# The bias of v folded into its weights, and the turn of x of batch 1 issued at other places: a linear-attention block with a feed-forward layer

## The chip, the cores and the metric

The kernel runs on one core of a Trainium2 chip. The metric is the device time of one execution in microseconds. A time is the median of several executions; the profile comes from one further execution, which has its own time and, inside it, its span from the first to the last instruction.

## The reference

All arithmetic is in float32. There are 8 batches of 1024 tokens with 256 channels; attention has 16 heads of 16 channels, and the hidden layer has 1024 channels.

```
xn  = (x - mean(x)) / sqrt(var(x) + 1e-5)              # over the 256 channels
q, k, v = split(xn @ qkv_w + qkv_b)                    # heads of 16
q, k = q / max(|q|, 1e-12), k / max(|k|, 1e-12)        # per token and head
kv  = sum over tokens of k[d] * v[e]                   # 16 x 16 per head
att = (q @ kv, heads joined) @ proj_w + proj_b
ffn = relu(xn @ W1 + b1) @ W2 + b2
out = x + att + ffn
```

There is no softmax. So the attention of a batch is `q` times one 256x256 matrix M = blockdiag(kv) @ proj_w, and the sum over tokens can be taken before the weights of v are applied.

## The kernel before, in words

Tokens lie on the 128 partitions in 8 tiles of 128 rows (`NT`); the 256 channels are two chunks of 128 (`KC`). The normalised x (`xn`, tokens on partitions, one buffer) is turned into `xnT` (channels on partitions, two buffers), which feeds the matmuls of the projections and of the hidden layer. The large products are split in 2x2 blocks and use seven block products in place of eight; the sums of blocks that this takes (`sums_of_a`, `sums_of_b`) are done by GpSimdE.

The program is written under a manual schedule: each engine gets its instructions in the order of the program text, and semaphores are set where data or buffers require them. The loop over batches `b` does, in this order: `hidden(b)` (first layer with relu, in 12 steps), `project(b + 1)` or `project_by_sums(b + 1)` (q and k of the next batch), and `second(b)` (second layer and `q @ M` in one accumulation), which is a generator in two parts, so that statistics, normalisation and turn of batch b + 2 and `mix_g(b + 1)` are issued between these parts.

The 12 steps of `hidden` (numbered from 0) are `first(0)`, `fifth(0)`, `first(1)`, `last(0)`, `fifth(1)`, `first(2)`, `last(1)`, `fifth(2)`, `first(3)`, `last(2)`, `fifth(3)`, `last(3)`. `first(i)` issues three block products into banks a, c, d, with a ScalarE copy `u1` and two VectorE adds; `fifth(i)` issues one into bank e with a VectorE add and a relu on ScalarE; `last(i)` completes a, d, e, with two VectorE adds and three relus. Behind each step the small work that a table names for it is issued: `first_steps` for batch 0 and `later_steps` for the others. In batch 0 this small work holds the whole normalisation of batch 1 (`norm_stats`, `norm_scale`, `norm_apply`), its turn (`turn_x`) and the mixing of batch 0.

The mixing of a batch has these parts. `sum_of_k` adds the normalised k over the tiles on GpSimdE, into `ksum` (128 x 256). `mix_g` forms G = xn^T k on TensorE (L492, `gp`) and copies it to `gT` on ScalarE. `mix_kv` forms v's side: for each of the two chunks a matmul of the bias of v with `ksum` (L505), and two of v's weights with `gT` (L509), all into `kvp`; VectorE then keeps the blocks of the heads. `mix_m` multiplies by proj_w.

`turn(dst, src, name, queues)` turns a 128 x 1024 pair of chunks in four parts: for each j a VectorE transpose of 32 x 32 blocks into a buffer (L291), and four transfers that move its row groups r to their places (L293). It is a generator, and `turn_x` issues one j for each call. A transfer is issued by an engine's queue, which stands still for that time. In the kernel before, the transfers of r = 1 and 3 are issued by ScalarE's queue for batch 1, and all others by SP:

```
turns["x", b] = turn(xnTs[b], xns[b], f"x_{b}", (nc.sync, nc.scalar if b == 1 else nc.sync))
```

The banks of PSUM are one pool of seven and one of one (for `gp`, `kvp`, `mp`).

Of the kernel before, what the change touches and what calls it, by code (L numbers as in the profile page):

```python
# [9 lines left out]
F32 = mybir.dt.float32  # L10
AF = mybir.ActivationFunctionType
ALU = mybir.AluOpType
# [4 lines left out]
def kernel(  # L17
# [10 lines left out]
    b2: bass.AP,  # L28
    out: bass.AP,
):  # L30

# [16 lines left out]
    nc = tc.nc  # L50
    P = 128
    B, N, C = x.shape
# [6 lines left out]
    KC = C // P  # L59
# [3 lines left out]
    R = P // S  # L63
# [5 lines left out]
    const = ctx.enter_context(tc.tile_pool(name="const", bufs=1))  # L69
    big = ctx.enter_context(tc.tile_pool(name="big", bufs=2))  # L70
    one = ctx.enter_context(tc.tile_pool(name="one", bufs=1))
# [20 lines left out]
    xs, xqs, xns, xnTs, xSs, hTs, qks, qTs, mixes, Ms, hSs = ({} for _ in range(11))  # L92
# [67 lines left out]
    make_identity(nc, ident)  # L160
    eps_sb = const.tile([P, 1], F32, tag="eps", name="eps_sb")
    nc.vector.memset(eps_sb, LN_EPS)

    blk = const.tile([P, G], F32, tag="blk", name="blk")
    nc.vector.tensor_reduce(blk, ident.rearrange("p (g d) -> p g d", d=D), AX.X, ALU.add)
# [69 lines left out]
    def norm_stats(b, tiles):  # L235

        xt, n = xs[b], len(tiles)
        st = work.tile([P, NT, 6], F32, tag="st", name=f"st_{b}_{tiles[0]}")[:, :n, :]
        mv = small.tile([P, NT, 2], F32, tag="mv", name=f"mv_{b}_{tiles[0]}")[:, :n, :]
        for i, t in enumerate(tiles):  # L240
            nc.vector.bn_stats(st[:, i, :], xt[:, t, :])
        for i in range(n):
            nc.vector.bn_aggr(mv[:, i, :], st[:, i, :])
        rstd = small.tile([P, NT], F32, tag="rstd", name=f"rstd_{b}_{tiles[0]}")[:, :n]
        nc.scalar.activation(rstd, mv[:, :, 1], AF.Sqrt, bias=eps_sb)
        for i, t in enumerate(tiles):
            stats[b, t] = i, mv, rstd

    def norm_scale(b, tiles, on_act):
        i, mv, rstd = stats[b, tiles[0]]  # L250
        nc.vector.reciprocal(rstd, rstd)
        if on_act:
            nmr = small.tile([P, NT], F32, tag="nmr", name=f"nmr_{b}_{i}")[:, : len(tiles)]
            nc.vector.scalar_tensor_tensor(nmr, mv[:, :, 0], -1.0, rstd, ALU.mult, ALU.mult)
            for t in tiles:
                stats[b, t] += (nmr,)
# [25 lines left out]
                    tp.rearrange("p (u w) m -> p u w m", w=2),  # L282
                )

    def turn(dst, src, name, queues=(nc.sync, nc.sync)):


        sq = one.tile([P, R, KC, NP, S, 2], F32, tag="turn", name=f"turn_{name}")
        src = src[:, :, 0:C].rearrange("p (u w) (k j s) -> p j k u w s", w=2, k=KC, s=S)
        for j in range(R):  # L290
            nc.vector.transpose(sq[:, j, :, :, :, :].rearrange("p k u s w -> p k u w s"), src[:, j])  # L291
            for r in range(R):
                queues[r % 2].dma_start(  # L293
                    out=dst[ts(j, S), :, :, ts(r, S), :], in_=sq[ts(r, S), j, :, :, :, :]
                )
            yield
# [3 lines left out]
    def turn_x(b):  # L300

        if b not in xnTs:
            xnTs[b] = big.tile([P, KC, NP, P, 2], F32, tag="xnT", name=f"xnT_{b}")
            turns["x", b] = turn(
                xnTs[b], xns[b], f"x_{b}", (nc.sync, nc.scalar if b == 1 else nc.sync)
            )
        next(turns["x", b])

    def project(b, between={}, with_norms=True):
# [164 lines left out]
            turns["q", b] = turn(qTs[b], qks[b], f"q_{b}")  # L474
        next(turns["q", b])

    def sum_of_k(b):
        qk = qks[b]

        ksum = one.tile([P, 2, C], F32, tag="ksum", name=f"ksum_{b}")  # L480
        nc.gpsimd.tensor_tensor(ksum, qk[:, 0:2, C : 2 * C], qk[:, 2:4, C : 2 * C], ALU.add)
        nc.gpsimd.tensor_tensor(ksum, ksum, qk[:, 4:6, C : 2 * C], ALU.add)
        nc.gpsimd.tensor_tensor(ksum, ksum, qk[:, 6:8, C : 2 * C], ALU.add)
        nc.gpsimd.tensor_tensor(ksum[:, 0], ksum[:, 0], ksum[:, 1], ALU.add)
        mixes[b] = [ksum]

    def mix_g(b):
        qk, xn = qks[b], xns[b]
        gp = ps_mix.tile([P, KC, C], F32, tag="mix", name=f"gp_{b}")
        for f in range(KC):  # L490
            for t in range(NT):
                nc.tensor.matmul(  # L492
                    gp[:, f, :], xn[:, t, ts(f, P)], qk[:, t, C : 2 * C],
                    start=(t == 0), stop=(t == NT - 1),
                )
        gT = one.tile([P, KC, C], F32, tag="gT", name=f"gT_{b}")
        nc.scalar.copy(gT, gp)
        mixes[b].append(gT)

    def mix_kv(b):  # L500
        ksum, gT = mixes.pop(b)
        kvp = ps_mix.tile([P, KC, P], F32, tag="mix", name=f"kvp_{b}")
        for c in range(KC):
            cols = slice(2 * C + c * P, 2 * C + (c + 1) * P)
            nc.tensor.matmul(  # L505
                kvp[:, c, :], qkvb_sb[:, cols], ksum[:, 0, ts(c, P)], start=True, stop=False
            )
            for f in range(KC):
                nc.tensor.matmul(  # L509
                    kvp[:, c, :], wqkv_sb[:, f, cols], gT[:, f, ts(c, P)],  # L510
                    start=False, stop=(f == KC - 1),
                )
        kvm = one.tile([P, KC, P], F32, tag="Mt", name=f"kvm_{b}")
        for c in range(KC):
            nc.vector.tensor_tensor(
                kvm[:, c, :].rearrange("p (g d) -> p g d", d=D),
                kvp[:, c, :].rearrange("p (g d) -> p g d", d=D),
                blk.unsqueeze(2).to_broadcast([P, G, D]), ALU.mult,
            )
        mixes[b] = kvm  # L520

    def mix_m(b):
        kvm = mixes.pop(b)
        mp = ps_mix.tile([P, KC, C], F32, tag="mix", name=f"mp_{b}")
        for c in range(KC):
            nc.tensor.matmul(mp[:, c, :], kvm[:, c, :], projw_sb[:, c, :], start=True, stop=True)  # L526
        M = one.tile([P, KC, C], F32, tag="M", name=f"M_{b}")
        Mt = one.tile([P, 3, HC], F32, tag="Mt", name=f"Mt_{b}")
        Ms[b] = M, Mt
        nc.vector.tensor_copy(M, mp)  # L530
        sums_of_b(
            nc.gpsimd, [M[:, k, ts(m, HC)] for k in range(2) for m in range(2)],
            [Mt[:, i, :] for i in range(3)],
        )
# [93 lines left out]
    def first_steps(b):  # L628

        lo, hi = range(HT), range(HT, NT)  # L630
        return {
            0: [lambda: load_squares(b)] + [lambda h=h: norms(b, h, all_ss[b, h]) for h in range(2)],
            1: [lambda: sum_of_k(b), lambda: norm_stats(b + 1, lo)],
            2: [lambda: norm_stats(b + 1, hi), lambda: norm_scale(b + 1, lo, True)],
            4: [
                lambda: mix_g(b), lambda: norm_scale(b + 1, hi, False),
                lambda: norm_apply(b + 1, lo), lambda: scale_q(b, 0), lambda: scale_q(b, 1),
            ],
            5: [lambda: norm_apply(b + 1, hi)],
            6: [lambda: mix_kv(b)],  # L640
            7: [lambda: turn_x(b + 1), lambda: turn_x(b + 1)],
            8: [lambda: turn_x(b + 1), lambda: turn_x(b + 1)],
            9: [lambda: mix_m(b)],
            11: [lambda: load(b + 2)],
        }

# [14 lines left out]
    def sums_of_q(b):  # L661
        sums_of_a(
            nc.vector if b == B - 1 else nc.gpsimd,
            halves(qTs[b]), *(hSs[b][:, s, FH] for s in range(3)),
        )
# [148 lines left out]
    for b in range(B):  # L814
        if b > 0:
            load_squares(b, (0,) if b == B - 1 else (0, 1))
            if b + 2 < B:
                load(b + 2)
        hidden(b)
        if b == 0:  # L820
            qTs[0] = one.tile([P, KC, NP, P, 2], F32, tag="qT", name="qT_0")
            turn_on_pe(qTs[0], qks[0], "q_0")
            sums_of_w2()
            sums_of_q(0)
        if b + 1 == 1:
            project(1)
            out_parts = second(b)
        elif b + 1 < B:
            project_by_sums(b + 1)
            out_parts = second(b, lambda: norms_of_q(b + 1))  # L830
        else:
            out_parts = second(b)
        next(out_parts)
        if b + 1 == 1:
            sums_of_x(1, 0)
            sums_of_x(1, 1)
            sums_of_wqk()
        if b + 1 < B:
            sum_of_k(b + 1)
        if b + 2 < B:  # L840
            norm_stats(b + 2, range(NT))
            norm_scale(b + 2, range(NT), True)
        if b + 1 < B:
            mix_g(b + 1)
        if b + 2 < B:
            norm_apply(b + 2, range(NT))
            for _ in range(R):
                turn_x(b + 2)
        next(out_parts)


# [29 lines left out]
```

## Time and profile before

| what | value |
|---|---|
| times of three executions, us | 627.03, 628.73, 628.95 (median 628.73) |
| the profiled execution: time, span, us | 626.93, 624.8 |
| TensorE matmul busy in the span | 616.5 us, 99% |
| VectorE busy | 399.7 us, 64% |
| GpSimdE busy | 385.4 us, 62% |
| ScalarE busy | 199.7 us, 32% |
| mean busy share of the 16 DMA engines on SP's and ScalarE's queue | 26.4% and 0.3% |
| granted TensorE clock | 0.999 |

PE is TensorE's matmul side, PEld its weight load, DVE VectorE, ACT ScalarE, POOL GpSimdE and SP the engine whose queue issues transfers. In a row, the arrow points from what is read to what is written, in the program's names; a count follows an x; in a timeline, the bracket tells how long the engine was idle before and what released it. In the chain of work that ended last, each row is a stretch of one engine that the end of the run depended on, with its start and length. Rows with "q" behind an engine are its queue, where transfers are issued. An f32 matmul of the program appears as two matmul records.

### The profile page before, as it was taken

Reading aid. Unit: us, or ns where it says so; the run is one execution under the profiler, and the core shown is the slowest. Engines: PE = TensorE matmul, PEld = TensorE weight load, DVE = VectorE, ACT = ScalarE, POOL = GpSimd, SP = SyncE. Lnnn points to the kernel's source line nnn. Section 1 sums busy time; section 2 is a strip of 40 time slices with the busy share of each in tenths; the row PEclk is TensorE's granted clock in tenths of the full one; section 3 lists DMA queues with packets and bytes.
Section 4 is the critical chain, followed back from the end, with each engine's and each line's share of the span. In section 5 each row is a group of like instructions: output and inputs, shape, how many; then the busy total and the mean of one; then the engine's idle time right before and its main releaser. Section 6 shows DMA issues by size and latency. Waiting matters only on the chain.

```text
span 624.8 us, 6180 instructions
## 1 busy us (share of the span) xinstructions
PE 616.5 (99%) x1873; PEld 348.0 (56%) x1873; DVE 399.7 (64%) x696; ACT 199.7 (32%) x340; POOL 385.4 (62%) x320
## 2 busy tenths in 40 slices
PE   8998999999999999999999999999999999999996
PEld 5464455556545666447564484644846557555454
DVE  6785725677647766577566874667845678417833
ACT  4354403352033521244231432315223252103500
POOL 3575949399534994259932797329954299543801
PEclk9999999999999999999999999999999999999999
DMA  7624001460015500264003710046100450004202
GB/s 254 118 58 134 3 0 29 124 175 11 0 50 134 154 2 0 65 156 117 0 1 100 190 47 0 5 123 175 36 0 22 122 125 2 0 1 101 67 1 67
DMA packets 139504, 43.28 MB, mean 69 GB/s; under 512 B 135880, under 2 KB 136272, under 8 KB 139472
## 3 DMA queue, kind: packets, MB, share of 16 engines
q1 hardware_dynamic: 137296, 42.37, 26.4%
q10 hardware_dynamic: 2176, 0.52, 0.3%
q8 instruction: 15, 0.25, 0.2%
q14 instruction: 17, 0.14, 0.1%
HBM read 19.80 MB, written 8.39 MB: 45 GB/s over the span
## 4 chain that ended last, share of the span: by engine, by line
PE 97%; DVE 1%; DMA 1%; ACT 0%; issue 0%; SPq 0%; ACTq 0%; DVEq 0%
PE poe L670 11%; PE poa L670 11%; PE pod L670 10%; PE gp L492 9%; PE phe L548 9%; PE pha L548 9%; PE phd L548 8%; PE poc L670 5%; PE pq L326 4%; PE phc L548 4%; PE pqa L394 3%; PE pqd L394 3%; PE pqe L394 3%; PE pqc L394 2%; PE kvp L509 1%; PE mp L526 1%
## 5 line engine op out<-in xcount | busy, mean ns | idle before, releaser
L707 POOL TENSOR_TENSOR xq<-xq,yt_o 128x512 f32<-128x512 f32 x30 | 37.9, 1264 | 145.0 <-DVE yt_o L702 145.0
L555 ACT ACTIVATE hT<-hT,b_sb 128x512 f32<-128x512 f32 x96 | 68.6, 721 | 60.3 <-DVE hT L560 55.7
L184 POOL TENSOR_TENSOR hS<-hT 128x512 f32<-128x512 f32 x31 | 46.5, 1499 | 60.7 <-ACT hT L555 60.7
L548 PE MATMUL pha<-xnT,w_sb 128*128 128x512 f32 x128 | 65.4, 592 | 0.0
L372 ACT ACTIVATE sq<-qk 128x512 f32<-128x512 f32 x48 | 29.0, 629 | 109.1 <-DVE qk L400 59.1
L670 PE MATMUL poa<-hT,w_sb 128*128 128x512 f32 x128 | 57.5, 592 | 0.0
L492 PE MATMUL gp<-qk,xn 128*128 128x256 f32 x256 | 56.6, 379 | 0.0
L492 PEld LDWEIGHTS gp<-qk,xn 128*128 128x128 f32 x256 | 48.6, 190 | 10.0 <-issue 3.8
L560 DVE TENSOR_TENSOR hT<-phe,u 128x512 f32<-128x512 f32 x64 | 43.7, 684 | 7.0 <-PE phe L548 5.3
L702 DVE STREAM_TRANSPOSE yt_o<-y_o 128x512 f32<-128x512 f32 x30 | 33.0, 1099 | 16.2 <-ACT y_o L757 13.9
L186 POOL TENSOR_TENSOR hS<-hT,hS 128x512 f32<-128x512 f32 x31 | 40.4, 1303 | 2.4
L185 POOL TENSOR_TENSOR hS<-hS,hT 128x512 f32<-128x512 f32 x31 | 40.3, 1299 | 2.4
L574 ACT COPY u<-pha 128x512 f32<-128x512 f32 x32 | 18.4, 575 | 69.5 <-PE pha L548 66.5
L188 POOL TENSOR_TENSOR hT<-hT 128x512 f32<-128x512 f32 x31 | 39.9, 1288 | 0.0
L670 PEld LDWEIGHTS poa<-hT,w_sb 128*128 128x128 f32 x128 | 24.3, 190 | 25.0 <-issue 24.4
L291 DVE STREAM_TRANSPOSE turn_x<-xn 128x512 f32<-128x512 f32 x28 | 17.6, 687 | 31.1 <-ACT xn L265 31.1
L548 PEld LDWEIGHTS pha<-xnT,w_sb 128*128 128x128 f32 x128 | 23.8, 190 | 23.8 <-issue 21.0
L560 DVE TENSOR_TENSOR u<-phc,u 128x512 f32<-128x512 f32 x32 | 21.8, 682 | 22.8 <-ACT u L574 15.0
L548 PE MATMUL phe<-xS,w_sb 128*128 128x512 f32 x64 | 32.8, 594 | 1.7 <-DVE hT L560 1.7
L555 ACT ACTIVATE hT<-pha,b_sb 128x512 f32<-128x512 f32 x32 | 21.8, 682 | 37.5 <-PE pha L548 32.4
L548 PE MATMUL phd<-xnT,w_sb 128*128 128x512 f32 x64 | 32.7, 592 | 0.0
L548 PE MATMUL phe<-xS,w1t 128*128 128x512 f32 x64 | 32.7, 592 | 0.0
(164 smaller groups left out, 1227.0 us busy)
## 6 DMA issues: line engine op xcount, KB each, us to landing
xq<-in_L_attn_x_dram SPq DMA_DIRECT2D x60, 128.0 KB, 3.0
out_dram<-xq SPq DMA_DIRECT2D x60, 128.0 KB, 2.4
x<-in_L_attn_x_dram SPq DMA_DIRECT2D x14, 512.0 KB, 6.6
qT<-turn_q SPq DMA_DIRECT2D x112, 64.0 KB, 2.1
xnT<-turn_x SPq DMA_DIRECT2D x104, 64.0 KB, 2.1
x<-in_L_attn_x_dram SPq DMA_DIRECT2D x4, 256.0 KB, 3.9
w_sb<-in_L_ffn_W_dram SPq DMA_DIRECT2D x2, 512.0 KB, 7.2
w_sb<-in_L_ffn_W_dram SPq DMA_DIRECT2D x8, 128.0 KB, 3.1
```

The lines of the kernel that those rows point to most:

```text
L184: eng.tensor_tensor(s1, a21, a22, ALU.add)
L185: eng.tensor_tensor(s2, s1, a11, ALU.subtract)
L186: eng.tensor_tensor(s4, a12, s2, ALU.subtract)
L188: eng.tensor_tensor(a21, a11, a21, ALU.subtract)
L394: nc.tensor.matmul(dst[:, w, :], a[:, g, :, w], rhs, start=start and w == 0, stop=stop, skip_group_check=True,)
L492: nc.tensor.matmul(gp[:, f, :], xn[:, t, ts(f, P)], qk[:, t, C : 2 * C], start=(t == 0), stop=(t == NT - 1),)
L548: nc.tensor.matmul(dst, lhsT, rhs, start=start, stop=stop, skip_group_check=True)
L555: nc.scalar.activation(block(i, n, m), src, AF.Relu, bias=b1_sb[:, fc : fc + 1])
L560: nc.vector.tensor_tensor(dst, p, q, ALU.add)
L670: nc.tensor.matmul(dst, l, r, start=start and n == 0, stop=stop and n == len(lhs) - 1, skip_group_check=True,)
L702: nc.vector.transpose(yt.rearrange("p u w r c -> p u r w c"), y.rearrange("p u (s r) w -> p u r w s", r=R),)
L707: nc.gpsimd.tensor_tensor(xh, xh, yt.rearrange("p u w r c -> p (u w) r c"), ALU.add)
```

## The change

The output is unchanged in meaning. A layer-normalised row sums to zero over its 256 channels. Let u be the vector with ones in the first 128 channels and zeros in the others. If 1 is added to the first 128 channels of `xn` (`shift`), `mix_g` forms G + u s^T, where s is the sum of k over the tokens. If a row `a` is added to every row of v's weights W (`fold_bias_of_v`), the product W'^T (G + u s^T) is W^T G + (W^T u + 128 a) s^T, because each column of G sums to zero over channels. With a = bias / 128 - (mean of the first 128 rows of W) this is W^T G + bias s^T, which is what the bias matmuls gave.

- `sum_of_k` and the two bias matmuls of each `mix_kv` are gone.
- `fold_bias_of_v` is issued once, behind step 3 of batch 0: a memset, one matmul and two VectorE instructions.
- `shift(b)` is one ScalarE activation over the first 128 channels of `xn`, issued once per batch: for batch 0 behind step 2, for batch 1 behind the turn of q on TensorE, for the later ones at the end of the loop's body, two batches ahead.
- The turn of x of batch 1 is issued one part behind step 7, two behind step 8 and one behind step 9 (two and two before), and only the transfer r = 3 of each part goes to ScalarE's queue.
- `mix_m` of batch 0 moves from behind step 9 to behind step 10.

```diff
+    ones = const.tile([P, 1], F32, tag="ones", name="ones")
+    nc.vector.memset(ones, 1.0)
...
-    def turn(dst, src, name, queues=(nc.sync, nc.sync)):
+    def turn(dst, src, name, last=nc.sync):
...
-                queues[r % 2].dma_start(
+                (last if r == R - 1 else nc.sync).dma_start(
...
-    def sum_of_k(b):
-        qk = qks[b]
-
-        ksum = one.tile([P, 2, C], F32, tag="ksum", name=f"ksum_{b}")
-        nc.gpsimd.tensor_tensor(ksum, qk[:, 0:2, C : 2 * C], qk[:, 2:4, C : 2 * C], ALU.add)
-        nc.gpsimd.tensor_tensor(ksum, ksum, qk[:, 4:6, C : 2 * C], ALU.add)
-        nc.gpsimd.tensor_tensor(ksum, ksum, qk[:, 6:8, C : 2 * C], ALU.add)
-        nc.gpsimd.tensor_tensor(ksum[:, 0], ksum[:, 0], ksum[:, 1], ALU.add)
-        mixes[b] = [ksum]
+    def fold_bias_of_v():
+
+        wv = wqkv_sb[:, :, of_v]
+        mean = one.tile([P, P], F32, tag="Mt", name="mean")
+        nc.vector.memset(mean, 1.0 / P)
+        of_rows = bank([P, C], "of_rows")
+        nc.tensor.matmul(of_rows, mean, wv[:, 0, :], start=True, stop=True)
+        a = one.tile([P, C], F32, tag="ksum", name="a")
+        nc.vector.scalar_tensor_tensor(
+            a, qkvb_sb[:, of_v], 1.0 / P, of_rows, ALU.mult, ALU.subtract
+        )
+        nc.vector.tensor_tensor(wv, wv, a.unsqueeze(1).to_broadcast([P, KC, C]), ALU.add)
+
+    def shift(b):
+
+        part = xns[b][:, :, 0:P]
+        nc.scalar.activation(part, part, AF.Identity, bias=ones)
...
     def mix_kv(b):
-        ksum, gT = mixes.pop(b)
+        gT = mixes.pop(b)
...
-            nc.tensor.matmul(
-                kvp[:, c, :], qkvb_sb[:, cols], ksum[:, 0, ts(c, P)], start=True, stop=False
-            )
...
-                    start=False, stop=(f == KC - 1),
+                    start=(f == 0), stop=(f == KC - 1),
...
-            1: [lambda: sum_of_k(b), lambda: norm_stats(b + 1, lo)],
-            2: [lambda: norm_stats(b + 1, hi), lambda: norm_scale(b + 1, lo, True)],
+            1: [lambda: norm_stats(b + 1, lo)],
+            2: [lambda: shift(b), lambda: norm_stats(b + 1, hi), lambda: norm_scale(b + 1, lo, True)],
+            3: [lambda: fold_bias_of_v()],
...
-            7: [lambda: turn_x(b + 1), lambda: turn_x(b + 1)],
+            7: [lambda: turn_x(b + 1)],
             8: [lambda: turn_x(b + 1), lambda: turn_x(b + 1)],
-            9: [lambda: mix_m(b)],
+            9: [lambda: turn_x(b + 1)],
+            10: [lambda: mix_m(b)],
...
             sums_of_q(0)
+            shift(1)
...
-        if b + 1 < B:
-            sum_of_k(b + 1)
...
         next(out_parts)
+        if b + 2 < B:
+            shift(b + 2)
```

More of the change, by code (lines that the diff above doesn't have):

```diff
@@ L303, in turn_x @@
             xnTs[b] = big.tile([P, KC, NP, P, 2], F32, tag="xnT", name=f"xnT_{b}")
-            turns["x", b] = turn(
-                xnTs[b], xns[b], f"x_{b}", (nc.sync, nc.scalar if b == 1 else nc.sync)
-            )
+            turns["x", b] = turn(xnTs[b], xns[b], f"x_{b}", nc.scalar if b == 1 else nc.sync)
         next(turns["x", b])
@@ L497, in mix_g @@
         nc.scalar.copy(gT, gp)
-        mixes[b].append(gT)
+        mixes[b] = gT
     def mix_kv(b):
-        ksum, gT = mixes.pop(b)
+        gT = mixes.pop(b)
         kvp = ps_mix.tile([P, KC, P], F32, tag="mix", name=f"kvp_{b}")
@@ L504, in mix_kv @@
             cols = slice(2 * C + c * P, 2 * C + (c + 1) * P)
-            nc.tensor.matmul(
-                kvp[:, c, :], qkvb_sb[:, cols], ksum[:, 0, ts(c, P)], start=True, stop=False
-            )
             for f in range(KC):
```

## The prediction

> **What bounds the kernel now.** I read the busy times first, then the chain of work that ended last, then TensorE's own waits.
>
> ```profile
> PE 616.5 (99%) x1873; PEld 348.0 (56%) x1873; DVE 399.7 (64%) x696; ACT 199.7 (32%) x340; POOL 385.4 (62%) x320
> PE 97%; DVE 1%; DMA 1%; ACT 0%; issue 0%; SPq 0%; ACTq 0%; DVEq 0%
> PE phe L548 <- DVE hT L560: 1.7, 1, 1.7
> ```
>
> TensorE is the bound: the chain is 97% PE, and after the start-up its only wait of size is one of 1.7 us. So a matmul taken out saves its time, and a matmul that waits costs its wait. The chain in order of time shows both places that the change touches:
>
> ```profile
> 44.83 0.22 PE kvp L505 x2
> 45.05 0.45 PE kvp L509 x4
> 45.50 0.22 PE kvp L505 x2
> 45.72 0.45 PE kvp L509 x4
> ...
> 47.89 1.22 DVE turn_x L291 x2
> ...
> 51.60 0.58 ACT u L574
> ...
> 57.33 1.12 PE phe L548 x2
> 58.45 1.75 PE tpq L279 x16
> 60.20 13.74 PE pq L326 x32
> ```
>
> First, the bias matmuls of `kvp` (L505) lie on the chain, 0.22 us each (an f32 matmul leaves two records). Secondly, batch 0's hidden stage leaves PE: a DVE turn, DMA issues on ScalarE, its copy `u` (L574), and DVE, until `phe` resumes at 57.33.
>
> The timeline of 24 to 75 us shows how far VectorE is behind TensorE where the new matmul is put:
>
> ```profile
> 31.75 1.02 PE L548 MATMUL phe<-xS,w1t 128*128 128x512 f32 x2
> 32.61 7.07 PE L492 MATMUL gp<-qk,xn 128*128 128x256 f32 x32
> 32.74 0.69 DVE L560 TENSOR_TENSOR u<-phc,u 128x512 f32<-128x512 f32 x1 [0.84 <-ACT u L574]
> 34.14 1.40 DVE L241 BATCH_NORM_STATS2 st<-x 128x6 f32<-128x256 f32 x4
> 36.73 1.27 DVE L560 TENSOR_TENSOR hT<-phe,u 128x512 f32<-128x512 f32 x2
> 38.01 4.20 DVE L462 TENSOR_TENSOR qk<-qk,ss 128x1024 f32<-128x1024 f32 x2
> ```
>
> TensorE ends `last(0)` at 31.91 (32.77 less the 0.86 us of `fifth(1)`); VectorE adds that step's `phe` only at 36.73 (the first of the two; the second is `fifth(1)`'s). The norm statistics of batch 1, put into steps 1 and 2, hold it up. Today nobody minds: `gp` needs nothing of it.
>
> **What the skill says.** "PSUM — Partial Sum Buffer", Engine vs sequencer instructions: the queues of ScalarE, VectorE and GpSimdE are strictly first in, first out, and matmuls keep program order. The trace agrees: every DVE row above stands in the order of the steps. "DMA: Bandwidth & Descriptors", Issuing engines are not separate DMA queues: a second issuing engine saves only issue time. Here that time is real, 0.68 us per turn transfer on SP:
>
> ```profile
> 103.49 10.93 SPq L293 DMA_DIRECT2D xnT<-turn_x  x16
> ```
>
> "TensorE: Matmul & The Clock Gate", What's actually happening: after an idle window of about 3.4 us the array runs at half speed until it has been busy for such a window. The start agrees, although the clock column says 1.00: 20 cold transposes take 226 ns apiece, 16 warm ones 109 ns by the chain (1.75/16). After the 1.7 us idle at 55.6, `tpq` was at full speed.
>
> ```profile
> 1.36 4.53 PE L786 MATMUL warm<-ident 128*128 128x128 f32 x20 [1.36 <-POOL ident masks.py:199]
> ```
>
> **The change part by part.**
>
> *Bias matmuls out.* Two per batch at 0.22 us: 0.44 x 8 = 3.5 us off PE. For batches 1 to 7 (3.1 us) PE shows no wait, so all of it counts.
>
> *Sum of kn out.* GpSimdE loses 1.27 x 3 + 0.73 = 4.5 us per batch. PE never waited on `ksum`, so this is worth nothing; the residual adds (L707) and stores come earlier, which the chain doesn't contain.
>
> *The fold, once, behind step 3 of batch 0.* It adds a memset of `mean` (DVE), a matmul `of_rows` of 256 columns (PE), then `a` and the add into `wv` (DVE). `of_rows` needs `mean`, and the memset stands in DVE's queue behind `last(0)`'s adds. These end 36.73 + 0.68 = 37.4, with the next issue about 0.6 us after the first, at 37.33. The memset of 128x128 isn't in the trace on DVE: between 0.15 us (reciprocal of 128x4) and 0.22 us (128x128 scalar op); I take 0.2. So PE, ready at 31.91, starts near 37.55 and sits idle 5.6 us with `fifth(1)` and `mix_g` behind it. `of_rows` takes 2 x 0.216 us (from 32 records of 256 columns in 6.91 us) and a restart of 0.26 (the `phe` after the wait took 1.12 instead of 0.86): it ends at 38.24. `fifth(1)` ends at 39.10, where it was 32.77: **+6.3 us**. The DVE part, 0.5 + 0.69 us (L772's and L560's rows), then runs beside `fifth(1)` and `gp`; VectorE has caught up, and its 4.2 us of `scale_q` fit under `gp`'s 6.9.
>
> Does the lateness of VectorE get paid back later by this pause? Only the wait at 55.6 could repay it, and that hangs on work behind `gp`: batch 1's normalised x reuses the single `xn` buffer, so ScalarE's copies of it (40.20 to 42.27) and its copy `u` at 42.18 follow `gp` as before. The delay carries through whole.
>
> *The array's clock.* An idle time of 5.6 us holds a whole free-running 3.4 us window with a chance of (5.6-3.4)/3.4 = 0.65. Half speed for one window costs 1.7 us. Bounds: 0, and half of the at most 5.7 us that the start was cold (1.36 to 7.05), 2.9. I take **+1.7**.
>
> *Shift.* Eight activations over 128x1024. By the trace an activation with a bias tile is 0.72 us at 512 elements; "ScalarE: Activation LUTs", What ACT_TABLE_LOAD costs, gives 280 ns + 0.833 ns per element, an estimate of 1.13 us; twice 0.72 is the upper bound. Batch 0's runs behind `u` (32.71) and ends near 33.9, under the wait for `mean`; without that wait `gp` would start 0.6 us late. Batch 1's stands behind the copies of `qT`, ahead of `project(1)`'s squares: these come 1.1 us later, with 1.1 us of ScalarE idle per tile (L332) to recover and seven banks released by DVE before them. Batches 2 to 7's wait for the last turn (105.1 in the first such stage) and end near 106.3; the next ScalarE work is at 111.84 after 8.7 us of idle. Zero.
>
> *Turn of x of batch 1.* Before: two turns behind step 7, two behind step 8, 8 transfers on SP, 8 on ScalarE. After: one, two, one, and only the fourth of each four on ScalarE, so SP issues 12. ScalarE's block ahead of `u` falls from 2.94 us to about 0.7. In the clock of before: turn 0 at 47.81, `u` at 49.3, DVE's two adds to 51.2, turns 1 and 2 to 52.5, `last(2)`'s adds to 53.7, turn 3 to 54.3, `fifth(3)`'s add to 54.9. TensorE, 0.44 us earlier by `kvp`, needs that add at 55.17: the 1.71 us wait goes. But then `tpq` ends at 57.8, and `project(1)` needs all 16 transfers. SP: three at 48.5 to 50.6, then nine from 51.9 at 0.68 us, the last issued at 57.3, landing 2.1 us later (their median): 59.4, perhaps 59.7. Before, `project(1)` began at 60.04. So 1.7 us are won and about 1.7 paid again for SP's queue; beyond the 0.44 of `kvp`, **0** (bounds -1.7 and +1). The move of `mix_m` behind step 10 is free: nothing needs M before the output stage.
>
> Sum: 6.3 + 1.7 - 3.5 + 0 = **+4.5 us**. Against the profiled execution (span 624.8, time 626.93) this is 631.4; that execution lies 1.8 under the median of the three runs, so against the median it is 633.2. With the clock spared it is 631.5.
>
> **Rivals.**
> *No wait for `mean`.* VectorE reaches the memset before PE needs it. Then `of_rows` costs 0.43, `gp` waits 0.6 for the shift, and the sum is 1.05 - 3.5 = -2.5 us: **626.2**. It decides as soon as VectorE is less than some 2 us behind at the end of `last(0)`. Against it: the 36.73 of the trace, and no earlier place in a first-in-first-out queue. For it: only that the issue order need not be that of the text.
>
> *The wait, but all else goes well.* The clock stays up and the transfers land before `tpq` ends: 6.3 - 3.5 - 1.7 = +1.1 us, **629.8**. For it: landing times as short as 2.0 us; against it: 12 issues at 0.68 are 8.2 us from 48.5.
>
> *SP worse than reckoned.* Transfers of two queues held each other up before (SP's fourth was issued 1.8 us late, put down to a transfer). Were that so with one ScalarE issue per turn, `project(1)` starts 1 to 2 us later still: **635**.
>
> **How the numbers follow.** Forecast 0.66 (with or without the clock penalty 631.5 to 634.5), worse SP 0.12, all going well 0.09, no wait 0.13. A difference of 0.3% (1.9 us) is about what can be told from none. Faster 0.13, same 0.09, slower 0.78. The range 629.7 to 635.6 leaves out the no-wait rival and the tails.
>
> **What would show it.** In the profile after: a PE wait of about 5.6 us at `of_rows`, released by the memset; `gp` of batch 0 starting near 39.1, or its first records at half speed; no L505 rows; the PE wait on L560 gone and a wait of `pq` on the turn's transfers in its place; stages of batches 1 to 7 of 74.8 us, where they were 75.3. I am wrong if `of_rows` runs straight behind `last(0)` at about 32 us.

## The result, and the profile after

| | before | after |
|---|---|---|
| median of six executions each, us | 627.06 (626.96 to 628.95) | 633.82 (633.43 to 635.73) |
| profiled execution: time, span, us | 626.93, 624.8 | 633.63, 631.8 |
| granted TensorE clock, mean over the span | 0.999 | 0.994 |

The kernel after is slower: the ratio of the times is 1.0105, with a 95% interval of 1.0086 to 1.0124, and the medians differ by 6.8 us. GpSimdE is busy for 349.0 us where it had 385.4 us, and 32 instructions fewer; TensorE's busy time is the same, although 16 bias matmuls are gone. The page, busy times of after:

```profile
PE 616.4 (98%) x1843; PEld 346.4 (55%) x1843; DVE 400.4 (63%) x700; ACT 208.8 (33%) x348; POOL 349.0 (55%) x288
```

A bound engine with less work and the same busy time has worked more slowly somewhere, and its span says that it has waited too. TensorE's waits in after (what waited, for what; us in total, times, the longest):

```profile
PE of_rows L485 <- DVE mean L483: 5.5, 1, 5.5
PE pq L328 <- DMA xnT<-turn_x: 1.9, 1, 1.9
```

The wait on VectorE's add (L560 before) is gone from this list. In its place stand one for the turn's transfers of about the same length, and a new one of 5.5 us. The chain of work that ended last, in order of time (start, length, engine, line), where the new wait lies:

```profile
36.41 1.28 DVE hT L567 x2
37.69 0.15 DVE mean L483
37.84 0.04 issue
37.88 1.22 PE of_rows L485 x2
39.10 1.71 PE phe L555 x2
40.81 8.29 PE gp L502 x32
```

The chain goes through VectorE's two late adds, then the memset, and only then to TensorE. And the matmuls behind it are slow: `phe` takes 1.71 us where it takes 0.86 elsewhere, `gp` 8.29 where it took 6.91. The table by stretches of time (stretch; its length; the busy time of PE, PEld, DVE, ACT and POOL, each with its instructions; then the granted clock, the DMA share and the rate) says why:

```profile
32.00:38.00 6.00, 0.45 (x2) 0.12 (x1) 4.85 (x20) 3.55 (x7) 0.76 (x2) 0.89 0.48 93
38.00:40.00 2.00, 2.00 (x4) 1.30 (x5) 0.83 (x2) 0.45 (x1) 1.92 (x2) 0.50 0.03 8
40.00:42.00 2.00, 2.00 (x5) 1.21 (x5) 2.00 (x4) 0.29 (x1) 1.92 (x2) 0.50 0.00 0
42.00:44.00 2.00, 2.00 (x8) 1.64 (x7) 2.00 (x2) 0.43 (x1) 2.00 (x2) 0.63 0.00 0
44.00:46.00 2.00, 2.00 (x11) 1.77 (x10) 1.49 (x1) 0.00 (x0) 0.41 (x1) 1.00 0.00 0
```

TensorE was busy for 0.45 of the 6 us from 32 on. Its clock fell to half before that wait was over, and came back between 42 and 44 (the trace's own record: half speed from 36.66, for 6.83 us). From 37.88 to 43.49 that is 5.6 us of matmuls at half speed, so about 2.8 us lost, an estimate from these two figures. The chain has 2.76 (the table below).

Later in the chain of after:

```profile
54.25 0.89 PE kvp L516 x8
...
66.74 2.14 DMA xnT<-turn_x
68.88 0.24 issue
69.12 13.98 PE pq L328 x32
```

`kvp` is 0.89 us for a batch where it was 1.34 (two rows of 0.22 fewer). `project(1)` starts at 69.12, released by the last transfer that SP issued. From the end of `gp` to the end of `project(1)` before took 34.26 us and after 34.00.

One more difference is in no wait of TensorE's: from the last VectorE add into x (L729 before, L738 after) to the end of the span it is 4.0 us before and 4.9 after. There the last stores land (the last row of each view below). The DMA view of before (a queue's packets, MB and share of 16 engines; then issues, KB each, median us to landing):

```profile
q1 hardware_dynamic: 137296, 42.37, 26.4%
...
xq<-in_L_attn_x_dram SPq DMA_DIRECT2D x60, 128.0 KB, 3.0
out_dram<-xq SPq DMA_DIRECT2D x60, 128.0 KB, 2.4
...
out_dram<-x SPq DMA_DIRECT2D x2, 256.0 KB, 2.5
```

The same view of after:

```profile
q1 hardware_dynamic: 138384, 42.63, 30.5%
...
xq<-in_L_attn_x_dram SPq DMA_DIRECT2D x60, 128.0 KB, 3.7
out_dram<-xq SPq DMA_DIRECT2D x60, 128.0 KB, 2.8
...
out_dram<-x SPq DMA_DIRECT2D x2, 256.0 KB, 3.5
```

Transfers of the same bytes took longer: the loads of `xq`, the stores of `xq`, and the two stores at the end. What the change did to them: the new constant `ones` (128 x 1) takes 32 bytes in each partition, and the buffers placed behind it move up by 32 bytes (`x` from 77568 to 77600, `xq` from 186112 to 186144, `xnT` from 61184 to 61216). Before, these addresses were multiples of 256.

The difference of the two spans, 7.0 us, in terms that the chains show one by one:

| term | us | from |
|---|---|---|
| first transfer of x lands later (3.58 us, not 3.16) | +0.4 | start of the chain; 2.7 to 3.8 in the runs below, with no order to it |
| TensorE idle for `mean` | +5.55 | idle time at `of_rows` |
| `of_rows` itself, with restart | +0.69 | taken as forecast, since here it ran at half speed (1.22 in all); 0.70 in the filler run below |
| `of_rows`, `phe` and `gp` at half speed | +2.76 | 1.22 + 1.71 + 8.29, less 0.69 + 0.86 + 6.91 |
| end of `gp` to end of `project(1)` | -0.26 | of it -0.44 `kvp`, so +0.18 for the turn; `project(1)` itself took 13.98 in place of 13.74 after its wait |
| end of `project(1)` to the last add | -3.12 | 546.92 before, 543.80 after: 7 x 0.446 |
| last add to the end | +0.95 | 4.9 less 4.0 |

### The profile page after: what moved, and what is told of

It reads as the page before. It is cut to its first block, busy times and chain, and to the rows that moved or that the text cites. A ratio compares the mean times of both kernels' runs of the same rounds, so it can differ in the third digit from the quotient of the medians.

```text
span 631.8 us, 6102 instructions
## 1 busy us (share of the span) xinstructions
PE 616.4 (98%) x1843; PEld 346.4 (55%) x1843; DVE 400.4 (63%) x700; ACT 208.8 (33%) x348; POOL 349.0 (55%) x288
## 4 chain that ended last, share of the span: by engine, by line
PE 94%; DVE 3%; DMA 1%; ACT 0%; issue 0%; SPq 0%; DVEq 0%; ACTq 0%
PE poe L679 11%; PE poa L679 11%; PE pod L679 10%; PE gp L502 9%; PE phe L555 8%; PE phd L555 8%; PE pha L555 8%; PE poc L679 5%; PE pq L328 4%; PE phc L555 4%; PE pqd L396 3%; PE pqe L396 3%; PE pqa L396 3%; PE pqc L396 2%; PE kvp L516 1%; PE mp L533 1%
## 5 line engine op out<-in xcount | busy, mean ns | idle before, releaser
L502 PE MATMUL gp<-qk,xn 128*128 128x256 f32 x256 | 58.0, 386 | 0.0
L190 POOL TENSOR_TENSOR hS<-hT,hS 128x512 f32<-128x512 f32 x31 | 39.9, 1286 | 2.4
L189 POOL TENSOR_TENSOR hS<-hS,hT 128x512 f32<-128x512 f32 x31 | 39.5, 1274 | 2.4
```

Source lines behind the costliest of these rows:

```text
L189: eng.tensor_tensor(s2, s1, a11, ALU.subtract)
L190: eng.tensor_tensor(s4, a12, s2, ALU.subtract)
L502: nc.tensor.matmul(gp[:, f, :], xn[:, t, ts(f, P)], qk[:, t, C : 2 * C], start=(t == 0), stop=(t == NT - 1),)
```

## The experiments

All were timed beside runs of the kernel before on the same chip. Before was 627.0 us in the first group (filler, memset early, turn alone, fold in `project(0)`), 626.98 in the second (ones beside eps, fold with the old turn, filler ahead of `project(1)`, two and two) and 626.99 in the third. A figure that compares one experiment with another, or with after, can go across these groups, whose before agrees to 0.02 us. The recorded mean clock of an execution, where it is given, also holds the half speed at the end of a program, when TensorE has no more work; that alone takes up to 0.003, as in the memset moved to the start (from 623.63 to its end at 627.14).

**Theory:** VectorE's lateness at `mean` and the clock lost to that wait make the kernel slow; the saving in `kvp` is real; the turn is about neutral; the stores at the end pay for the place of `ones`. **Rivals:** the stall would have come anyway a little later (a bank, or an add at 55 us), so that the wait is repaid; the slow matmuls are not the clock; the transfers are slow for another reason than their addresses.

### The wait alone, put into the kernel before

```diff
+    def wait_for_memset():
+        mean = one.tile([P, P], F32, tag="Mt", name="mean")
+        nc.vector.memset(mean, 1.0 / P)
+        of_rows = bank([P, C], "of_rows")
+        nc.tensor.matmul(of_rows, mean, wqkv_sb[:, 0, of_v], start=True, stop=True)
+        a = one.tile([P, C], F32, tag="gT", name="a")
+        nc.vector.tensor_copy(a, of_rows)
...
+            3: [wait_for_memset],
```

> The kernel before with only the memset of mean, the matmul of_rows and a copy of its result (not used) behind step 3; the bias matmuls, ksum and the turn stay. Theory (wait and clock are the whole loss): 5.5 us idle, 0.7 for the matmul and its restart, 2.8 for the clock, together 9 us over before. Rival (the later lateness of VectorE is paid back by the pause): 7 us or less, with the wait of phe on VectorE's add gone.

Measured: 636.12 us, ratio 1.0136 (1.0118 to 1.0153), so 9.1 us. Its chain, and then TensorE's waits:

```profile
37.38 0.15 DVE mean L489
...
37.57 1.22 PE of_rows L491 x2
38.79 1.71 PE phe L556 x2
40.50 7.76 PE gp L500 x32
```

```profile
PE of_rows L491 <- DVE mean L489: 5.7, 1, 5.7
PE phe L556 <- DVE hT L568: 1.6, 1, 1.6
```

The same `of_rows` and `phe` as in after, to 0.01 us. And the wait on VectorE's add of before is still there with 1.6 us: nothing of the pause is paid back. The rival, 7 us or less without that wait, is out.

The size needs care. The table's terms give 5.55 + 0.69 + 2.76 = 9.0 us, and the median of these four executions agrees with it. The profiled one is the fastest of the four (635.21, its span 8.4 us over that of before), and its own terms are 5.65 us idle, 0.69 for `of_rows`, and 2.23 for the clock, 8.6 together: `gp` took 7.76 here and 8.29 in after. The half speed lasted 6.83 us in both, but here it began earlier, at 35.28, so that 2.3 us of it fell into the wait where after had 1.2. So the price of the clock depends on when the half speed starts.

### TensorE kept busy through the wait

```diff
         of_rows = bank([P, C], "of_rows")
+        for i in range(48):
+            nc.tensor.transpose(of_rows[:, 0:P], ident, ident)
         nc.tensor.matmul(of_rows, mean, wv[:, 0, :], start=True, stop=True)
```

> As after, but TensorE runs 48 transposes of the identity into the bank of of_rows while it would wait for the memset (48 x 0.109 = 5.2 us); they compute nothing. Theory (the idle time also costs clock): of_rows still starts at about 37.9 us, but gp takes 6.9 us in place of 8.3 and the stretch from of_rows to the end of gp is 2.8 us shorter; 2.8 us under after. Rival (the slow stretch is due to VectorE, GpSimdE and TensorE reading SBUF together): no change against after.

Measured: 630.69 us, ratio to before 1.006 (1.0044 to 1.0076), 3.1 us under after. Its chain:

```profile
37.39 0.15 DVE mean L483
...
37.58 0.70 PE of_rows L487 x2
38.28 0.86 PE phe L557 x2
39.14 6.91 PE gp L504 x32
```

`mean` is as late as in after, but TensorE is busy until 0.3 us before it, and everything behind runs at full speed. So `gp` was slow because of the clock, not because VectorE and GpSimdE read the memory beside it: during `gp` they are busy for 4.75 and 5.80 us here, and for 4.68 and 3.60 in after. From `of_rows` to the end of `gp` it is 8.47 us in place of 11.22, so the clock was worth 2.75 us; 0.3 of the 3.1 is an earlier start of `of_rows`.

### The memset at the start of the program

```diff
     nc.vector.memset(ones, 1.0)
+    mean = one.tile([P, P], F32, tag="Mt", name="mean")
+    nc.vector.memset(mean, 1.0 / P)
...
-        mean = one.tile([P, P], F32, tag="Mt", name="mean")
-        nc.vector.memset(mean, 1.0 / P)
         of_rows = bank([P, C], "of_rows")
```

> The memset of mean is issued at the start of the program, the rest is as in the kernel after. Theory (the position in VectorE's queue is the cost): the 5.5 us wait of of_rows goes, and with it the 2.8 us at half clock. Left of it: fifth(1) may wait until about 33.9 us for a PSUM bank, since of_rows now holds one that a VectorE instruction frees late (1 to 2 us). Forecast 1 to 2.5 us under before, 8 us under after. Rival (of_rows waits for a PSUM bank that ScalarE's relu or VectorE frees near 37 us, and the memset only happened to come at that time): of_rows still waits about 5 us and the time stays within 1 us of after.

Measured: 628.98 us, ratio 1.0027 (1.002 to 1.0035): 4.8 us under after, but not under before, which was expected. Its waits on TensorE:

```profile
PE pq L330 <- DMA xnT<-turn_x: 3.2, 1, 3.2
...
PE phe L555 <- DVE u L567: 1.1, 1, 1.1
```

The wait at `of_rows` is gone. `fifth(1)` then waits 1.1 us for a bank that VectorE frees, and `gp` runs from 34.69 at full speed. What was missed lies at `project(1)`: it waits 3.2 us for the turn's transfers and its 32 matmuls take 15.68 us where before needed 13.74. That is the clock again: half speed from 63.84, for 3.41 us, which is 1.7 of the 1.94 us (the rest also shows in after, where `pq` takes 13.98 after a wait at full clock). The turn is not neutral once the pause ahead of it is gone.

### The turn alone

```diff
-                queues[r % 2].dma_start(
+                (last if r == R - 1 else nc.sync).dma_start(
...
-            7: [lambda: turn_x(b + 1), lambda: turn_x(b + 1)],
+            7: [lambda: turn_x(b + 1)],
             8: [lambda: turn_x(b + 1), lambda: turn_x(b + 1)],
-            9: [lambda: mix_m(b)],
+            9: [lambda: turn_x(b + 1)],
+            10: [lambda: mix_m(b)],
```

> The kernel before with only the turn's part of the change (one, two, one; one ScalarE transfer in four; mix_m behind step 10). Theory of the prediction (the wait moves from VectorE's add to SP's queue): within 0.5 us of before; the 1.7 us wait on VectorE's add is gone and project(1) waits 1.2 to 2 us for the transfers. Rival (the turn's part is worth its 1.7 us, and the fold alone spoils the change): 1.7 us under before, with no wait of project(1).

Measured: 629.32 us, ratio 1.003 (1.0016 to 1.0043), so 2.3 us, where at most 0.5 was expected. Its chain, and then the waits of SP's queue:

```profile
58.41 2.05 DMA xnT<-turn_x
60.45 0.24 issue
60.70 15.68 PE pq L324 x32
```

```profile
SPq L293 <- DVE turn_x L291: 15.5, 2, 14.4
SPq L293 <- DMA xnT<-turn_x: 2.1, 2, 1.1
```

TensorE's wait for VectorE's add is gone, as the prediction had it, and `project(1)` starts at 60.70 where it started at 60.20. To that 0.5 come 1.94 us for the slower `pq` (half speed from 60.9, for 3.41 us): 2.4 us, and so do the spans differ.

The fourteen times fall into groups, and the clock recorded for each execution goes with them: five at 627.4 to 627.8 with a mean clock of 0.998 to 1.000, nine at 629.1 to 631.7 with 0.992 to 0.997. So where the clock is kept, the turn costs the 0.5 us that was expected; what the prediction lacked is that its wait mostly costs the clock.

By the second SP row SP stands still for a transfer, twice, up to 1.1 us. Before has this row too (2.9 us in two waits, the longest 1.8). The trace names the semaphore that each transfer signals when it lands. These programs use eight for both queues, 101 to 108, and an issue that needs one which is still in use waits until that transfer has landed. ScalarE's first transfer is issued with number 106 at 48.53 and has landed at 50.90; SP's third needs 106 too, and is issued only at 50.91. So the split of a turn over two queues can make one of them wait for the landing of the other's.

### The fold inside project(0)

```diff
-            2: [lambda: shift(b), lambda: norm_stats(b + 1, hi), lambda: norm_scale(b + 1, lo, True)],
-            3: [lambda: fold_bias_of_v()],
+            2: [lambda: norm_stats(b + 1, hi), lambda: norm_scale(b + 1, lo, True)],
...
-    project(0, {HT - 2: second_half}, False)
+    project(0, {HT - 2: second_half, 4: fold_bias_of_v, 5: lambda: shift(0)}, False)
```

The memset stands at the start of the program, as above; the turn is that of after.

> As after, but mean is set at the start, the fold is issued behind tile 4 of project(0) and the shift of batch 0 behind tile 5, where VectorE and ScalarE keep up with TensorE. Theory: no wait at all for the fold; 0.43 us for its matmul, 3.5 us saved by the bias matmuls, and the turn's 1.9 us wait as in after: 3 us under before, about 9.5 under after. Rival (the DVE instructions of the fold make VectorE later in the hidden stage and TensorE waits there): within 1 us of before.

Measured: 627.55 us, ratio 1.0003 (0.9992 to 1.0013), where 3 us under before was expected. No matmul waits for the fold, and `gp` starts at 33.28. The gain is lost where it was lost with the memset early: `pq` waits 3.2 us and takes 15.67. Its fourteen times fall into two groups, three at 625.9 to 626.1 and eleven at 627.3 to 628.8. The middles of the groups are 1.7 us apart, about what the clock costs. The recorded mean clock is 0.999 in the lower three and 0.992 to 0.997 in ten of the upper eleven, but 1.000 in one of these (627.28). So the clock accounts for most of the upper group and not for all of it; only one execution has a profile (627.47, clock lost).

### The fold, with the turn of before

```diff
-    eps_sb = const.tile([P, 1], F32, tag="eps", name="eps_sb")
+    eps_ones = const.tile([P, 2], F32, tag="eps", name="eps_ones")
+    eps_sb, ones = eps_ones[:, 0:1], eps_ones[:, 1:2]
...
-            turns["x", b] = turn(xnTs[b], xns[b], f"x_{b}", nc.scalar if b == 1 else nc.sync)
+            turns["x", b] = turn(
+                xnTs[b], xns[b], f"x_{b}", (nc.sync, nc.scalar if b == 1 else nc.sync)
+            )
```

This is the fold inside `project(0)`, with `ones` as a second column of the tile that holds epsilon, and with the steps and queues of the turn, and `mix_m`, as before.

> The fold alone, placed in project(0), mean set at the start, ones beside eps, and the turn and mix_m of batch 1 as in the kernel before. Theory: 0.43 us for the matmul of the fold, 3.5 us saved by the bias matmuls, the 1.7 us wait on VectorE's add as before: 3.1 us under before, no loss of clock. Rival (the fold hardly pays, the matmuls left take their time): within 1 us of before.

Measured: 624.25 us, ratio 0.9957 (0.9943 to 0.9972). It is 2.7 us under before and has the lowest median of all, though its interval overlaps with those of the next two below. TensorE's first wait is the one that before has, on VectorE's add:

```profile
PE phe L557 <- DVE hT L569: 2.0, 1, 2.0
```

An idle time of 2.0 us left the clock up, and `project(1)` starts without a wait. So, but for 0.4 us, the fold does bring what the bias matmuls cost (8 x 0.44 less one `of_rows` of 0.43 us: 3.1), once nothing waits for it and the turn is left alone. The profiled execution is above the median (626.27): there the clock was at half from 8.63, for 3.41 us, in `project(0)`, ahead of the fold and of the turn. The fold inside `project(0)` and the filler ahead of `project(1)` have the same memset at the start and kept the clock there, so this loss is not put down to the edit.

### The new turn, with TensorE kept busy ahead of project(1)

```diff
             turn_on_pe(qTs[0], qks[0], "q_0")
+            fill = bank([P, P], "fill")
+            for i in range(28):
+                nc.tensor.transpose(fill, ident, ident)
```

The rest is the fold inside `project(0)` with `ones` beside epsilon, and the turn of after.

> As the fold in project(0) with the turn of after (the fourth run), ones beside eps, and 28 transposes of the identity (3 us of work that computes nothing) on TensorE behind the turn of q, where it would wait for the transfers of x. Theory (the idle time before project(1) costs the clock as well): project(1) starts as late as without them, and its 32 records take 13.8 us in place of 15.7; with 0.8 us for the place of ones, 2.7 us under the fourth run, 2.5 us under before. Rival (project(1) was slow because transfers and GpSimdE read SBUF at the time): only the 0.8 us.

Measured: 624.7 us, ratio 0.9963 (0.995 to 0.9976), 2.85 under the same without the filler and with `ones` in a tile of its own (the place of `ones` is worth 0.9 of that, as shown below). Its chain:

```profile
56.66 1.75 PE tpq L285 x16
58.41 3.06 PE fill L833 x28
61.47 13.74 PE pq L330 x32
```

`project(1)` starts no earlier than without the filler (61.48), yet its 32 matmuls take 13.74 us in place of 15.67. So 1.9 us of the new turn's loss is the clock that goes with the idle time; the late transfers themselves stay late, and this kernel is not shown to be faster than the fold with the turn of before.

### Two attempts at a better turn

Both stand on the fold inside `project(0)`, with `ones` beside epsilon.

```diff
             7: [lambda: turn_x(b + 1), lambda: turn_x(b + 1)],
             8: [lambda: turn_x(b + 1), lambda: turn_x(b + 1)],
-            9: [lambda: turn_x(b + 1)],
             10: [lambda: mix_m(b)],
```

> The fold in project(0), ones beside eps, and the turn of batch 1 with two parts behind step 7 and two behind step 8, one ScalarE transfer in four, mix_m behind step 10. Theory (SP's queue sets the start of project(1)): SP issues turns 0 and 1 in one go, without the 1.3 us gap behind turn 0, so that the last transfer is issued near 56.6 us and project(1) waits about 1 us in place of 3.2 and keeps its clock; ScalarE's copy u comes 0.7 us later and phe of last(3) may wait 0.5 us. 3.5 us under before, the fastest so far. Rival (two ScalarE issues ahead of u bring the 1.7 us wait back): as the fold with the old turn, 3.1 us under before.

Measured: 625.25 us, ratio 0.9973 (0.9962 to 0.9984), 1.7 under before where 3.5 was expected. The profiled execution, at the top of its times (628.43), waits 2.6 us at `project(1)` and loses the clock there, and it had lost it once before, from 8.48 in `project(0)`. It is not typical: five of the nine executions are at 624.6 to 625.3 with a mean clock of 0.998 to 1.000, the other four at 626.5 and above with 0.994 to 0.997. SP stood still from 51.98 to 53.08 and from 55.66 to 57.46, each time for a semaphore that ScalarE's transfer had just taken.

```diff
-                (last if r == R - 1 else nc.sync).dma_start(
+                (last if r % 2 and j < 2 else nc.sync).dma_start(
```

> The fold in project(0), ones beside eps, and the turn of batch 1 as one, two, one parts, with r = 1 and 3 of the parts 0 and 1 on ScalarE and all others on SP. In this order no transfer of SP takes a semaphore that a transfer of ScalarE has just taken. Theory (each transfer uses one of eight semaphores, in turn, and an issue waits until the last transfer with the same one has landed; that is what held SP in the earlier runs): SP waits for no landing, issues its last transfer near 58 us, project(1) waits 1.5 us and keeps its clock; 3.2 us under before. Rival (SP's pauses come from the transfers themselves): pauses of 1 us remain and project(1) waits 2.5 us or more; 1 to 2.5 us under before.

Measured: 626.65 us, ratio 0.9981 (0.9973 to 0.9989). As meant, SP issues its ten transfers from 53.32 without a pause, the last at 59.42. But the two issues on ScalarE push the copy `u` to 50.57, and with it the next parts of the turn:

```profile
PE pq L330 <- DMA xnT<-turn_x: 2.5, 1, 2.5
...
PE phe L555 <- DVE hT L567: 0.7, 1, 0.7
```

Half speed follows from 61.89. So SP's pauses did come from the semaphores, but one wait was exchanged for another. Ten of the 22 executions are at 625.0 to 625.5 with a mean clock of 0.998 to 1.000, twelve at 626.6 to 627.3, and nine of these have 0.995 to 0.997. Neither version was shown to beat the turn of before.

### The place of `ones`

In the kernel before, an added tile that nothing uses:

```diff
+    ones = const.tile([P, 1], F32, tag="ones", name="ones")
+    nc.vector.memset(ones, 1.0)
```

> The kernel before with one unused tile of 128x1 and its memset ahead of blk; nothing else is changed. It moves x, xq, xnT and the turn's buffer by 32 bytes. Theory (the place of the tiles costs): landings of xq 3.6 us in place of 3.0, of the last stores 3.4 in place of 2.5, and 0.5 to 1 us over before. Rival: no change (within 0.2 us).

Measured: 627.88 us, ratio 1.001 (1.0002 to 1.0019), so 0.9 us. Its DMA view:

```profile
q1 hardware_dynamic: 137296, 42.37, 30.5%
...
xq<-in_L_attn_x_dram SPq DMA_DIRECT2D x60, 128.0 KB, 3.7
out_dram<-xq SPq DMA_DIRECT2D x60, 128.0 KB, 2.8
```

These are the landings and the queue's share of after, in a program that is otherwise that of before; the last two stores land in 3.3 us (before 2.5). The last add ends at 620.90 (before: 620.86), and the time behind it is 4.8 us. The reverse, in the kernel after:

```diff
-    eps_sb = const.tile([P, 1], F32, tag="eps", name="eps_sb")
+    eps_ones = const.tile([P, 2], F32, tag="eps", name="eps_ones")
+    eps_sb, ones = eps_ones[:, 0:1], eps_ones[:, 1:2]
...
-    ones = const.tile([P, 1], F32, tag="ones", name="ones")
```

> As after, but ones is the second column of eps's tile, so that no tile behind it is moved: in the kernel after the tile of ones (4 bytes, padded to 32) moves x, xq, xnT, the turn's buffer and others 32 bytes up, to places that are not multiples of 64. Theory (the place costs the transfers time): landing of xq and of the last stores goes back from 3.7 and 3.5 us to 3.0 and 2.5, the stretch from the last add to the end of the span from 4.9 to 4.0 us; 0.8 to 1 us under after. Rival (landings vary by themselves from program to program): unchanged.

Measured: 633.28 us, ratio to before 1.0095 (1.0081 to 1.011). The landings are back at 3.0 and 2.4 us, and the time behind the last add is 3.95 us, 0.95 less than in after. The median falls only by 0.5, which these intervals do not tell from none; the profile shows the effect, the times of this run (four executions) do not. That the place of the buffers is the cause is shown by the tile added to before.

"DMA: Bandwidth & Descriptors", How a descriptor splits into AXI transactions, says that a transaction has to start at a multiple of 256 bytes, and that a descriptor which does not start there costs extra. The direction and the sixty rows of either kind agree; how many of the packets are cut was not measured, and no shift other than 32 bytes was tried, so the multiple of 256 as the reason is argued, not shown.

## Why the prediction was right, and where not

*Right in its mechanism.* Slower, because TensorE stands at `of_rows` for a memset behind VectorE's late adds: 5.6 us forecast, 5.55 measured, and the memset took 0.165 us inside its bounds of 0.15 to 0.22. `of_rows` with its restart: 0.69 forecast, 0.70 with the filler. Nothing of the delay is repaid: shown by the wait put alone into the kernel before. The bias matmuls: 3.5 us forecast, 3.56 measured, all of it on the path (stages of 74.8 us where they had 75.3, as forecast). The sum of kn: worth nothing, 36.4 us of GpSimdE's time gone without a trace in the chain. The shift: 1.15 us each where 1.13 was estimated, never on the chain.

*The clock was too small.* The step took one window at half speed with a cost of 1.7 us, bounds 0 and 2.9. It was two such stretches (6.83 us), begun 1.2 us before the wait ended, and cost 2.76 us. The step failed in letting half speed end after one window. In the first one, 36.66 to 40.07, TensorE was busy for only 2.19 us, and the clock stayed down through the next. The step also took the loss to need a whole window without work, with a chance of 0.65; in the turn alone 2.5 us of idle time were enough.

*The turn was right in after only.* The step had a wait of 1.7 us gone, and 1.7 paid again for SP's queue. In after that is what happened (1.9 us at `pq`, and +0.18 us in all). But its bound of +1 is too low for the edit as such: alone it costs 2.3 us by the medians. The step counted SP's issues at 0.68 us each, which is near enough (0.61 us, and up to 0.1 between them), and left out two things: that the issues wait on each other's semaphores, which it had seen in before and named only as a rival, and that an idle time of 2.5 us costs the clock again. Without the clock the edit costs 0.5 us, inside the bound.

*A term was missing.* The place of `ones`: +0.95 us at the end. The working looked at instructions, and not at what an added tile does to the addresses of all others.

*The total agreed by luck.* The forecast of 633.2 is near the 633.82 measured. But it stood on a median of three runs, 628.73, where six give 627.06, 1.7 us lower: two of those three were among the longer times of before (of 90 executions timed later, 13 lie above 628.3 and the rest at 626.8 to 627.6). The sum was +4.5 us where the spans differ by 7.0. Of the 2.5 us short, 1.06 is the clock, 0.95 the end, 0.4 the first transfer and 0.18 the turn. The too high start and the too small sum nearly cancelled. The estimate counted from the profiled execution, 631.4, is the fairer measure of the working, and it is 2.4 us under the measured median.

The rivals: "no wait for `mean`" is refuted by the 5.5 us; "the wait, but all else goes well" by the half-speed records; "SP worse" did not hold in after, but its mechanism is what the turn alone shows.

## What to carry to other kernels

Before a matmul is put into a stream, look in the timeline how far behind the engine is that makes its operand, and make the operand where that engine is idle: the same fold cost 6.8 us with the rest of its change, and gained 2.7 us when done in `project(0)`, with the turn left alone and `ones` beside epsilon. Price a TensorE wait of over 2 us as the wait and the clock, and keep the array busy with throw-away work if it can't be avoided. Where the times of a kernel fall into groups, look at the clock recorded for each execution before trusting a median of few. Put a new small constant into a tile that exists, or see that the addresses of the large buffers stay where they were.

## What the runs showed of the hardware

- **How long an idle time costs the clock.** In the profiled executions TensorE kept its full clock over waits of 1.7 us (before), 1.9 (after), and 2.0 (filler, fold with the old turn). It lost it at 2.5 (turn alone, two queues early), 2.6 (two and two), 3.2 (memset early, fold in `project(0)`) and 5.5 us (after). "TensorE: Matmul & The Clock Gate", What's actually happening, speaks of an idle window of about 3.4 us. The length of the half-speed stretches agrees (3.41 us, or two of them), but 2.5 us of idle time were enough here.
- **How much work in a window keeps it.** Lay windows of 3.41 us through each trace so that the recorded changes of clock stand on their borders. Around the end of batch 0's `hidden`, where these programs wait, the last window at full speed held 0.92 us of matmuls in the turn alone, and 0.64 to 0.91 in the four other traces with a wait of 2.5 to 3.2 us; the clock fell. It held 1.43 us in the fold with the old turn and 1.70 in before; the clock stayed. So the border at this place lies between 0.92 and 1.43 us of work. This rule does not carry to the start of a program: in the fold with the old turn and in two and two the clock fell at 8.63 and 8.48 although the window before held 2.1 and 2.4 us of matmuls, mostly small transposes, while 2.3 us kept it in the fold inside `project(0)` and in the filler ahead of `project(1)`. Why is open.
- **Eight semaphores join the queues of these programs.** An issue on SP can wait 1.0 to 1.8 us for the landing of a transfer that ScalarE issued, if their numbers coincide. In before it stands at 52.31, 1.8 us late: it needs 101, which ScalarE's transfer of 50.22 gives free at 52.29. In after they did not coincide: ScalarE's first transfer had 101, SP's first three 108, 102 and 103. Moving one transfer changes this for all later ones.
- **VectorE beside GpSimdE.** The add of `a` into the weights of v was taken as 0.69 us and took 1.48. The timeline of after shows what ran beside it:

```profile
39.27 1.26 POOL L189 TENSOR_TENSOR hS<-hS,hT 128x512 f32<-128x512 f32 x1
39.59 1.48 DVE L490 TENSOR_TENSOR wqkv_sb<-wqkv_sb,a 128x512 f32<-128x512 f32 x1
...
40.61 1.59 POOL L190 TENSOR_TENSOR hS<-hT,hS 128x512 f32<-128x512 f32 x1
```

GpSimdE's L189 ends at 40.53 and the add 0.54 us later. The same add took 0.71 us in the fold with the old turn, where GpSimdE's instruction ended 0.16 us after its start, 0.96 in the fold inside `project(0)` (0.42), 1.38 with the filler ahead of `project(1)` (0.83), and 1.69 with the memset early (1.15). In each it ended 0.54 to 0.55 us after that instruction, as if it did its work only then. L190, which began while the add ran, took 1.59 us where the mean of its line is 1.29. "SBUF — State Buffer", Who interferes with whom, says that a VectorE instruction with two inputs in SBUF contends with GpSimdE's reads, and these times fit that. It cost nothing in after, since TensorE was in `gp`.
